# Moving small steps of a transformer layer between VectorE, GpSimd and ScalarE: the rotary product, the high halves and the pair sums

## The chip, the core and the metric

The kernel runs on one core of a Trainium2 chip. The metric is the device time of one execution, in microseconds. Before the change three runs gave 1519.38, 1523.75 and 1528.3 us; their median is 1523.75 us. The engines are called by the names of the profile: PE is TensorE (PEld its weight loads), DVE is VectorE, ACT is ScalarE, POOL is GpSimd, SP is the engine that issues most DMAs.

## The reference

The input x has 2 x 1024 rows of 1024 values, in f32. The reference computes one layer in three steps, each on a layer norm of what came before:

```
x = x + 0.5 * ffn(layernorm(x))
x = x + attention(layernorm(x))
x = x + 0.5 * ffn(layernorm(x))        # the same weights as the first ffn

ffn(x):       base = x @ base_w.T + base_b
              gate = top 2 of 8 experts by x @ gate_w.T, weights by softmax of the two
              low  = x @ lora_A[e].T            (rank 16, all 8 experts)
              base + 2 * sum_e gate[e] * low[e] @ lora_B[e].T
attention(x): q = x @ Wq (32 heads of 32), k = x @ Wk, v = x @ Wv (8 heads of 32)
              q, k = rotary(q), rotary(k):  q * cos + rotate_half(q) * sin
              softmax(causal(q k^T / sqrt(32))) v, four q heads to one k head, then @ Wo
```

## The kernel before

**Precision.** PE multiplies in f16. Each f32 operand is written as a high half (the value rounded to f16) and a low half (what is left, in f16), and a product is the sum of three matmuls: high by high, high by low, low by high (`dense`, L361 to L363). The halves are made on the vector engines. For a normed row tile this is `Split.add`: the high half is a copy (L311 on ACT for the first two tiles' first norm, L313 on POOL for all others), the low half a subtraction on DVE (L314), and a transposing DMA issued by SP brings both to the layout that PE needs (L317). For q and k the halves stand side by side in one tile, so that one matmul over 96 rows sums all three products: `kv_out` writes high, low and again high (L499 to L501), `q_out` high, high and low (L510 to L512), and the second high half is a DVE copy of the first.

**Tiles and stages.** There are 16 row tiles of 128 rows, 8 to a batch entry. Each passes through four stages: `stage_a1` (norm, first FFN, norm), `stage_a2` (k and v, then q in two parts, with the rotary step `rope`), the attention of its 8 key heads, `stage_c1` (output projection, norm) and `stage_c2` (second FFN, store). The base weights of the FFN stay on the chip; those of the attention are split once, written to DRAM (`wstr`) and streamed back in pieces by DMAs from SP (L373).

**The attention of a tile.** For each key head g, `unit_s1` makes scores of all 4 query heads against each key tile j (L575, three accumulators) and takes their row maxima on DVE (L592); the maxima are put into the query tile, and a transposing DMA (`qt_load`, L555) brings it to PE. `unit_s2` then makes the transposed scores (L695, two accumulators), and ACT takes the exponential (L701, tile `p32`, 8 buffers). For the diagonal tile POOL sets the masked part to zero (L703). The sums of two neighbouring exponentials (`pair`, L710, 2 buffers) serve the denominator. `av_add` collects up to `BATCH` = 4 exponentials; when `SKEW` = 2 further ones have been made, `av_batch` issues the batch's products with the values and with ones (L641, accumulator `av`). The last batch of a head is divided out by L648 to L657.

**Order.** The dense stages are Python generators that yield after every two steps of k, that is six matmuls. `step` runs the attention of a tile slot by slot, and after each slot takes dense pieces from the stages planned beside it, so many that `npieces` (from `SIZE`) are used up by the end of the tile; what is left over is issued at its end. The order of emission is a priority: a scheduler at build time places the instructions of each engine by it and by its own timing, and the engines run their queues strictly in that order. Two things bind it further: dense instructions stand on PE behind the score product some steps back (`behind`), and the matmuls of one batch in `av_batch` stand in a chain of their own. At the start, `piece`, `pow2` and `split` (L169 to L195) prepare the weights on ACT, DVE and POOL while the first tiles run.

**The lines that the change touches.** In `rope` ACT copies the accumulator to `qs` (L468), DVE makes the product with the cosine from `qs` (L472), POOL the two products with the sine (L477, L481), and DVE adds (L485). In `ffn` the accumulator of the base and expert products is finished by L445, and DVE adds it to the residual tile `xt` (L446). Two accumulators (`p_dense`) serve all dense products.

Of the kernel before, what the change touches and what calls it, by code (L numbers as in the profile page):

```python
# [19 lines left out]
P = 128  # L20
# [19 lines left out]
def kernel(  # L40
# [256 lines left out]
    class Split:  # L297
# [4 lines left out]
            self.tt = tp.tile([P, 2 * KB, P], HP, name="tt")  # L302
            self.n, self.done = n, 0

        def add(self, src, act=False):

            w, i = D // self.n, self.done
            src = src[:, i * w : (i + 1) * w]
            hi = self.hl[:, 2 * i * w : (2 * i + 1) * w]
            if act:  # L310
                nc.scalar.copy(hi, src)  # L311
            else:
                nc.gpsimd.tensor_scalar(hi, src, 1.0, 0.0, ALU.mult, ALU.add)  # L313
            nc.vector.tensor_tensor(self.hl[:, (2 * i + 1) * w : (2 * i + 2) * w], src, hi, ALU.subtract)  # L314
            m = 2 * KB // self.n
            pin(
                nc.sync.dma_start_transpose(  # L317
                    out=self.tt[:, i * m : (i + 1) * m, :], in_=self.hl[:, 2 * i * w : (2 * i + 2) * w]
                )
            )  # L320
            self.done += 1
# [6 lines left out]
            m = KB // self.n  # L328
            return self.tt[:, k // m * 2 * m + m + k % m, :]

    def layernorm(xt, act=False, n=1):
# [12 lines left out]
        rs = small.tile([P, 1], FP, name="rs")  # L344
        nc.vector.tensor_tensor(rs, n1, r, ALU.mult)
        nb = small.tile([P, 1], FP, name="nb")
        nc.vector.scalar_tensor_tensor(nb, mv[:, 0:1], -1.0, rs, ALU.mult, ALU.mult)
        xn = fpool.tile([P, D], FP, name="xn")
        sp = Split(n)
        for i in range(n):  # L350
            c = bass.ts(i, D // n)
            nc.scalar.activation(xn[:, c], xt[:, c], AF.Identity, bias=nb, scale=rs)
            sp.add(xn, act)
        return sp

    def dense(ps, tt, wsel, n=512, last=True):
# [36 lines left out]
    def ffn(xt, tt, done):  # L393
# [34 lines left out]
        for n in range(2):  # L428
# [14 lines left out]
            nc.tensor.matmul(ps, lhsT=lh, rhs=lbh[:, c], start=False, stop=False)  # L443
            nc.tensor.matmul(ps, lhsT=lh, rhs=lbl[:, c], start=False, stop=False)
            nc.tensor.matmul(ps, lhsT=ll, rhs=lbh[:, c], start=False, stop=True)  # L445
            nc.vector.scalar_tensor_tensor(xt[:, c], ps, S["uf", n], xt[:, c], ALU.mult, ALU.add)  # L446
            done(n)
            if n == 0:
                yield True

    def stage_a1(t):
        tt = layernorm(xts[t], t < 2)
        yield

        def done(n):
# [9 lines left out]
    def rope(ps, n, nh, i):  # L465
# [6 lines left out]
        nc.vector.tensor_tensor(  # L472
            t1.rearrange("p h (a d) -> p (h a) d", a=2),
            qs.rearrange("p h (a d) -> p (h a) d", a=2),
            cosT[:, i, :].unsqueeze(1).to_broadcast([P, 2 * nh, H]), ALU.mult,
        )
        nc.gpsimd.tensor_tensor(  # L477
            t2[:, :, 0:H], qs[:, :, H:DH],
# [11 lines left out]
    def kv_out(t, ps):  # L490
# [7 lines left out]
        ks = kst  # L498
        nc.scalar.copy(ks[:, :, 0:DH], k1)  # L499
        nc.vector.tensor_tensor(ks[:, :, DH : 2 * DH], k1, ks[:, :, 0:DH], ALU.subtract)  # L500
        nc.vector.tensor_copy(ks[:, :, 2 * DH : 3 * DH], ks[:, :, 0:DH])  # L501
        kt = kts[:, (t + TPB) % (TPB + 1)]
        nc.sync.dma_start_transpose(out=kt, in_=ks.rearrange("p g c -> p (g c)"))
        KT[t] = kt
# [1 line left out]
    def q_out(t, n, ps):  # L506
# [2 lines left out]
        h = slice(n * 16, n * 16 + 16)  # L509
        nc.scalar.copy(qs[:, h, 0:DH], q1)  # L510
        nc.vector.tensor_tensor(qs[:, h, 2 * DH : 3 * DH], q1, qs[:, h, 0:DH], ALU.subtract)
        nc.vector.tensor_copy(qs[:, h, DH : 2 * DH], qs[:, h, 0:DH])  # L512
# [99 lines left out]
    class Context:  # L612
# [8 lines left out]
        def low(self, k):  # L621
            return self.tt[:, KB + k, :]

    def av_batch():

        t, g, L, us = pend.popleft()
        if us[0][0] == 0:
            avt[0] = p_av.tile([P, 2, P], FP, name="av")
        av = avt[0]
        last = us[-1][0] == L - 1  # L630
        runs = [(0, VA[t - t % TPB + j][:, g, :], p32) for j, p32, _ in reversed(us)]
        runs += [(1, ones, sums) for _, _, sums in reversed(us) if sums is not None]
        prev = None
        for n, (i, w, p32) in enumerate(runs):
            for h in range(GRP):
# [22 lines left out]
            if g == NKV - 1:  # L658
                CT[t] = CTX.pop(t)

    def av_add(t, g, j, L, p32, sums):

        if not pend or len(pend[-1][3]) == BATCH or pend[-1][0:2] != (t, g):
            pend.append((t, g, L, []))
        pend[-1][3].append((j, p32, sums))
        after = 0
        while len(pend) > 1:
            after = sum(len(b[3]) for b in list(pend)[1:])
            if after < SKEW:
                break  # L670
            av_batch()
# [15 lines left out]
    def unit_s2(t, g):  # L687
# [5 lines left out]
        for j in range(L):  # L693
# [8 lines left out]
            if j == L - 1:  # L702
# [1 line left out]
                    out=p32, in_=p32, compare_op=ALU.is_ge, fill=0.0, base=0,  # L704
                    pattern=[[0, GRP], [1, P]], channel_multiplier=-1,
                )
            sums = None
            if j % 2 == 1:
                sums = pp.tile([P, GRP, P], FP, name="pair", bufs=2)
                nc.vector.tensor_tensor(sums, even, p32, ALU.add)  # L710
            elif j == L - 1:
                sums = p32
            even = p32
            av_add(t, g, j, L, p32, sums)
            yield

    def stage_c1(t):
# [312 lines left out]
```

## Time and profile before

| | |
|---|---|
| median of 3 runs | 1523.75 us (1519.38 to 1528.3) |
| profiled execution | 1522.31 us, of which the span from first to last instruction is 1520.5 us |
| mean granted clock of PE | 0.973 |
| busy: PE, DVE, ACT, POOL | 1396.4, 1182.2, 687.9, 518.3 us |
| instructions: PE, DVE, ACT, POOL | 14548, 2468, 1280, 711 |
| HBM | 181.63 MB read, 20.45 MB written, 133 GB/s over the span |

A busy time is the union of the instructions' own durations; an engine that waits in its queue for a semaphore is idle. Matmuls are pipelined and their ends are modelled, so a busy PE is not a PE at its peak. The clock is what the throttle granted to PE, as a share of full speed. The chain that ended last is followed back from the last instruction, at each step to what released it or to the instruction before it on its engine. Lines are those of the kernel before; durations of single groups come from the one profiled execution.

### The profile page before, as it was taken

How to read it: one execution, taken by the hardware profiler on the slowest of the kernel's cores; microseconds unless marked ns; L12 is line 12 of the kernel's file. 1: busy time of each engine (PE TensorE's matmuls, PEld its weight loads, DVE VectorE, ACT ScalarE, POOL GpSimd, SP SyncE). 2: the span in 40 equal slices, each digit the busy share in tenths (PEclk: the TensorE clock that was granted, in tenths of full speed). 3: DMA queues.
4: the chain of work that ended last, by engine and by line, in shares of the span. 5: the costliest groups of instructions: out<-in, count | busy, mean ns of one | idle time of the engine just before them, and what ended most of it. 6: DMA issues, size and time to landing. Idle time of an engine off the chain costs nothing.

```text
span 1520.5 us, 35288 instructions
## 1 busy us (share of the span) xinstructions
PE 1396.4 (92%) x14548; PEld 781.8 (51%) x14548; DVE 1182.2 (78%) x2468; ACT 687.9 (45%) x1280; POOL 518.3 (34%) x711
## 2 busy tenths in 40 slices
PE   3687699799999999998999899989999999999998
PEld 2343345465555555555644445545555555556544
DVE  6877668786969799688864777877879799799653
ACT  7453325353545445454542334433545445465530
POOL 3443224523424334132232434433424232321231
PEclk9898899999999999999999999999999999999999
DMA  9967778849383753834646769657483854923551
GB/s 278 309 180 156 159 242 213 259 118 298 72 290 76 220 169 57 271 98 85 212 143 193 216 198 267 174 150 245 95 279 66 232 151 85 270 71 85 133 174 42
DMA packets 293074, 267.29 MB, mean 176 GB/s; under 512 B 258480, under 2 KB 261552, under 8 KB 272432
## 3 DMA queue, kind: packets, MB, share of 16 engines
q1 hardware_dynamic: 289360, 252.45, 60.5%
q10 hardware_dynamic: 3552, 12.58, 2.4%
q8 instruction: 114, 1.87, 0.5%
q14 instruction: 48, 0.39, 0.1%
HBM read 181.63 MB, written 20.45 MB: 133 GB/s over the span
## 4 chain that ended last, share of the span: by engine, by line
PE 59%; DVE 18%; DMA 9%; issue 3%; POOL 3%; ACT 2%; SPq 1%; ACTq 0%; DVEq 0%; POOLq 0%
PE pd L361 12%; PE pd L362 12%; PE pd L363 12%; PE av L641 10%; PE s L695 6%; PE s L575 6%; DVE mx L592 5%; DMA ws<-wstr 4%; DMA qt<-qst 3%; DVE pair L710 3%; DVE hl L314 2%; DVE o L650 2%; DMA wstr<-ws 1%; ACT p L701 1%; DVE ws L195 1%
## 5 line engine op out<-in xcount | busy, mean ns | idle before, releaser
L701 ACT ACTIVATE p<-s,cs 128x512 f32<-128x512 f32 x576 | 381.3, 687 | 265.1 <-PE s L695 261.5
L592 DVE TENSOR_REDUCE mx<-s 128x4 f32<-128x512 f32 x480 | 314.6, 676 | 60.4 <-PE s L575 36.4
L575 PE MATMUL s<-kts,qt 96*128 96x128 f16 x2304 | 219.6, 222 | 25.4 <-DMA qt<-qst 12.7
L361 PE MATMUL pd<-ws,tt 128*128 128x512 f16 x592 | 225.9, 382 | 11.6 <-DMA ws<-wstr 9.5
L710 DVE TENSOR_TENSOR pair<-p,p 128x512 f32<-128x512 f32 x256 | 190.5, 747 | 56.3 <-ACT p L701 25.8
L695 PE MATMUL s<-qt,kts 128*128 128x512 f16 x576 | 210.9, 385 | 21.9 <-DMA qt<-qst 15.1
L575 PEld LDWEIGHTS <-qt 96*128 96x128 f16 x2304 | 166.9, 99 | 120.8 <-issue 35.7
L362 PE MATMUL pd<-ws,tt 128*128 128x512 f16 x592 | 225.7, 381 | 0.0
L363 PE MATMUL pd<-ws,tt 128*128 128x512 f16 x592 | 225.0, 381 | 0.0
L361 PE MATMUL pd<-wb,tt 128*128 128x512 f16 x512 | 197.4, 386 | 7.7 <-DVE xt L446 6.1
L362 PEld LDWEIGHTS <-tt 128*128 128x128 f16 x1360 | 134.5, 99 | 134.5 <-issue 26.2
L363 PEld LDWEIGHTS <-tt 128*128 128x128 f16 x1360 | 134.4, 99 | 129.1 <-issue 6.3
L361 PEld LDWEIGHTS <-tt 128*128 128x128 f16 x1360 | 134.6, 99 | 125.6 <-issue 16.3
L362 PE MATMUL pd<-wb,tt 128*128 128x512 f16 x512 | 196.9, 385 | 0.4 <-DVE wb L195 0.4
L363 PE MATMUL pd<-wb,tt 128*128 128x512 f16 x512 | 196.3, 383 | 0.0
L641 PE MATMUL av<-p,va 128*32 128x128 f32 x4608 | 167.2, 279 | 2.5 <-ACT o L648 1.9
L703 POOL TENSOR_SCALAR_AFFINE_SELECT p<-p 128x512 f32<-128x512 f32 x128 | 91.8, 720 | 226.0 <-ACT p L701 222.3
L657 POOL TENSOR_TENSOR tt<-o,tt 128x128 f16<-128x128 f32 x128 | 62.7, 490 | 277.2 <-ACT tt L656 266.9
L641 PEld LDWEIGHTS av<-p,va 128*32 128x32 f32 x4608 | 116.1, 110 | 62.3 <-issue 48.0
L650 DVE RECIPROCAL o<-o 128x128 f32<-128x128 f32 x128 | 120.6, 943 | 15.9 <-ACT o L648 15.7
L587 POOL TENSOR_SCALAR_AFFINE_SELECT sm<-sm 128x512 f32<-128x512 f32 x96 | 66.3, 690 | 139.5 <-ACT sm L586 136.9
L398 POOL TENSOR_TENSOR xt<-xt,bb 128x512 f32<-128x512 f32 x64 | 106.0, 1677 | 0.0
(178 smaller groups left out, 1840.0 us busy)
## 6 DMA issues: line engine op xcount, KB each, us to landing
ws<-wstr SPq DMA_DIRECT2D x148, 1024.0 KB, 5.8
wstr<-ws ACTq DMA_DIRECT2D x9, 1024.0 KB, 6.5
xt<-in_x_dram SPq DMA_DIRECT2D x16, 512.0 KB, 4.5
out_dram<-xt SPq DMA_DIRECT2D x15, 512.0 KB, 2.7
ws<-in_wb_dram SPq DMA_DIRECT2D x2, 1024.0 KB, 8.0
qst<-in_wb_dram SPq DMA_DIRECT2D x2, 1024.0 KB, 7.5
st<-in_wo_dram SPq DMA_DIRECT2D x2, 1024.0 KB, 11.2
kts<-in_wo_dram SPq DMA_DIRECT2D x2, 1024.0 KB, 12.3
```

The source lines that it names most:

```text
L361: nc.tensor.matmul(ps, lhsT=th, rhs=wh, start=(k == 0), stop=False)
L362: nc.tensor.matmul(ps, lhsT=th, rhs=wl, start=False, stop=False)
L363: nc.tensor.matmul(ps, lhsT=tl, rhs=wh, start=False, stop=(last and k == KB - 1))
L398: nc.gpsimd.tensor_tensor(xt[:, c], xt[:, c], bb[:, c], ALU.add)
L575: nc.tensor.matmul(ps[:, h, :], lhsT=q[0 : 3 * DH, h, :], rhs=KT[b0 + j][0 : 3 * DH, g, :], start=(not pem or h == 0), stop=not pem,)
L592: nc.vector.tensor_reduce(mx[:, odd, j, :], ps, AX.X, ALU.max)
L641: prev = nc.tensor.matmul(av[rows, i, :], lhsT=w, rhs=p32[:, h, :], start=(us[0][0] == 0 and n == 0), stop=(last and n == len(runs) - 1), ...
L650: nc.vector.reciprocal(rc, rc)
L695: ins = nc.tensor.matmul(ps.rearrange("p h k -> p (h k)"), lhsT=KT[b0 + j][:, g, :], rhs=q.rearrange("p h k -> p (h k)"), start=True, stop ...
L701: nc.scalar.activation(p32, ps, AF.Exp, scale=cs)
L703: nc.gpsimd.affine_select(out=p32, in_=p32, compare_op=ALU.is_ge, fill=0.0, base=0, pattern=[[0, GRP], [1, P]], channel_multiplier=-1,)
L710: nc.vector.tensor_tensor(sums, even, p32, ALU.add)
```

## The change

Five things are changed, and the computed function stays the same.

1. In `Split.add` the high half is always copied by ACT; the choice of the engine (`act`) is gone.
2. In `rope` the cosine product reads the accumulator itself and scales by 2^-23 in the same DVE instruction. ACT's scaled copy `qs` stays for the sine products.
3. In `kv_out` and `q_out` the second high half is an ACT copy of the rotated product, in place of a DVE copy of the first high half.
4. The pair sums are no longer made right after their second exponential. `add_pairs` makes all sums of a batch together, when the first exponential of the next batch has been made, or at the latest in `av_batch`. An odd exponential at the end of a head goes to the denominator by itself, as before.
5. In `ffn` there is a `yield` more, between the last expert matmul and the residual update, for each of the two halves. The counts in `SIZE` are as before.

No edges of order are added for any of this.

```diff
-        def add(self, src, act=False):
+        def add(self, src):
...
-            if act:
-                nc.scalar.copy(hi, src)
-            else:
-                nc.gpsimd.tensor_scalar(hi, src, 1.0, 0.0, ALU.mult, ALU.add)
+            nc.scalar.copy(hi, src)
             nc.vector.tensor_tensor(self.hl[:, (2 * i + 1) * w : (2 * i + 2) * w], src, hi, ALU.subtract)
...
             nc.tensor.matmul(ps, lhsT=ll, rhs=lbh[:, c], start=False, stop=True)
+            yield
             nc.vector.scalar_tensor_tensor(xt[:, c], ps, S["uf", n], xt[:, c], ALU.mult, ALU.add)
...
-        nc.vector.tensor_tensor(
+        nc.vector.scalar_tensor_tensor(
             t1.rearrange("p h (a d) -> p (h a) d", a=2),
-            qs.rearrange("p h (a d) -> p (h a) d", a=2),
-            cosT[:, i, :].unsqueeze(1).to_broadcast([P, 2 * nh, H]), ALU.mult,
+            ps.rearrange("p (h a d) -> p (h a) d", a=2, d=H), 2.0**-23,
+            cosT[:, i, :].unsqueeze(1).to_broadcast([P, 2 * nh, H]), ALU.mult, ALU.mult,
         )
...
-        nc.vector.tensor_copy(ks[:, :, 2 * DH : 3 * DH], ks[:, :, 0:DH])
+        nc.scalar.copy(ks[:, :, 2 * DH : 3 * DH], k1)
...
-        nc.vector.tensor_copy(qs[:, h, DH : 2 * DH], qs[:, h, 0:DH])
+        nc.scalar.copy(qs[:, h, DH : 2 * DH], q1)
...
+    pairs = {}
+
+    def add_pairs(batch):
+
+        t, g, L, us = batch
+        key = (t, g, us[0][0])
+        if key in pairs:
+            return
+        pairs[key] = []
+        for i in range(0, len(us), 2):
+            if i + 1 == len(us):
+                pairs[key].append(us[i][1])
+                continue
+            sums = pp.tile([P, GRP, P], FP, name="pair", bufs=2)
+            nc.vector.tensor_tensor(sums, us[i][1], us[i + 1][1], ALU.add)
+            pairs[key].append(sums)
+
     def av_batch():
 
+        add_pairs(pend[0])
         t, g, L, us = pend.popleft()
...
-        runs += [(1, ones, sums) for _, _, sums in reversed(us) if sums is not None]
+        runs += [(1, ones, sums) for sums in reversed(pairs.pop((t, g, us[0][0])))]
...
         while len(pend) > 1:
             after = sum(len(b[3]) for b in list(pend)[1:])
+            add_pairs(pend[0])
             if after < SKEW:
                 break
             av_batch()
...
-            sums = None
-            if j % 2 == 1:
-                sums = pp.tile([P, GRP, P], FP, name="pair", bufs=2)
-                nc.vector.tensor_tensor(sums, even, p32, ALU.add)
-            elif j == L - 1:
-                sums = p32
-            even = p32
-            av_add(t, g, j, L, p32, sums)
+            av_add(t, g, j, L, p32)
             yield
```

More of the change, by code (lines that the diff above doesn't have):

```diff
@@ L329, in low, with layernorm @@
             return self.tt[:, k // m * 2 * m + m + k % m, :]
-    def layernorm(xt, act=False, n=1):
+    def layernorm(xt, n=1):
         st = small.tile([P, 2, 6], FP, name="bst")
@@ L352, in layernorm @@
             nc.scalar.activation(xn[:, c], xt[:, c], AF.Identity, bias=nb, scale=rs)
-            sp.add(xn, act)
+            sp.add(xn)
         return sp
@@ L451, in stage_a1 @@
     def stage_a1(t):
-        tt = layernorm(xts[t], t < 2)
+        tt = layernorm(xts[t])
         yield
@@ L630, in av_batch @@
         last = us[-1][0] == L - 1
-        runs = [(0, VA[t - t % TPB + j][:, g, :], p32) for j, p32, _ in reversed(us)]
-        runs += [(1, ones, sums) for _, _, sums in reversed(us) if sums is not None]
+        runs = [(0, VA[t - t % TPB + j][:, g, :], p32) for j, p32 in reversed(us)]
+        runs += [(1, ones, sums) for sums in reversed(pairs.pop((t, g, us[0][0])))]
         prev = None
@@ L659, in av_batch, with av_add @@
                 CT[t] = CTX.pop(t)
-    def av_add(t, g, j, L, p32, sums):
+    def av_add(t, g, j, L, p32):
         if not pend or len(pend[-1][3]) == BATCH or pend[-1][0:2] != (t, g):
             pend.append((t, g, L, []))
-        pend[-1][3].append((j, p32, sums))
+        pend[-1][3].append((j, p32))
         after = 0
```

## The prediction

> **What bounds the kernel now.** I read four views. First the page: busy time of each engine, and the chain that ended last.
>
> ```profile
> PE 1396.4 (92%) x14548; PEld 781.8 (51%) x14548; DVE 1182.2 (78%) x2468; ACT 687.9 (45%) x1280; POOL 518.3 (34%) x711
> ...
> PE 59%; DVE 18%; DMA 9%; issue 3%; POOL 3%; ACT 2%; SPq 1%; ACTq 0%; DVEq 0%; POOLq 0%
> ```
>
> PE is the engine that the end waits for, with DVE second: 18% of the chain is 274 us (0.18 x 1520.5), while ACT, on which the change puts work, carries 2% (30 us). Next the windows of 100 us (columns: busy of PE, PEld, DVE, ACT, POOL, then granted clock), because the 8% that PE lacks is not spread evenly.
>
> ```profile
> 0.00:100.00 100.00, 62.79 (x307) 32.08 (x308) 75.60 (x203) 59.32 (x94) 39.18 (x74) 0.90 0.91 270
> 100.00:200.00 100.00, 73.40 (x524) 36.60 (x523) 71.67 (x161) 38.01 (x70) 36.89 (x49) 0.86 0.70 148
> ...
> 400.00:500.00 100.00, 98.96 (x1142) 56.82 (x1135) 84.68 (x171) 49.72 (x93) 39.88 (x50) 1.00 0.58 162
> ```
>
> The first 200 us lack 64 us of PE, at a granted clock of 0.90 and 0.86; in the middle PE is at 99% and nothing that happens on DVE or ACT can be worth much there. Third, what PE itself waited for (engine, line, releaser: total us, times, longest).
>
> ```profile
> PE s L575 <- DVE mx L592: 12.1, 21, 3.4
> ...
> PE s L695 <- ACT p L701: 6.4, 12, 2.1
> PE pd L361 <- DVE xt L446: 6.3, 3, 3.6
> PE s L436 <- DVE lw L421: 5.8, 3, 3.0
> ...
> PE av L641 <- DVE pair L710: 3.3, 8, 1.4
> ```
>
> The whole list comes to about 119 us; 27 us of it are DVE's attention and expert work above, 28 are the query transposes (`DMA qt<-qst`, 15.1 and 12.7), 9.5 the streamed weights, 33 the scale set-up at the start (L174 and L445 on L179, untouched). So what a lighter DVE can give is bounded by some 30 us plus what hangs behind it. Fourth, the groups by line and shape (busy us, mean ns, idle before it and its releasers), for the prices.
>
> ```profile
> L701 ACT ACTIVATE p<-s,cs 128x512 f32<-128x512 f32 x576 | 381.3, 687 | 265.1 <-PE s L695 261.5 <-DVE pair L710 0.7 <-POOL p L703 0.6
> L710 DVE TENSOR_TENSOR pair<-p,p 128x512 f32<-128x512 f32 x256 | 190.5, 747 | 56.3 <-ACT p L701 25.8 <-PE av L641 20.7 <-POOL p L703 9.5
> L314 DVE TENSOR_TENSOR hl<-xn,hl 128x1024 f16<-128x1024 f32 x48 | 81.8, 1704 | 13.3 <-POOL hl L313 13.3
> L313 POOL TENSOR_SCALAR hl<-xn 128x1024 f16<-128x1024 f32 x46 | 50.3, 1093 | 91.2 <-ACT xn L352 91.2
> L446 DVE SCALAR_TENSOR_TENSOR xt<-pd,uf,xt 128x512 f32<-128x512 f32 x64 | 46.9, 737 | 24.8 <-PE pd L445 24.4
> L472 DVE TENSOR_TENSOR t<-qs,cosT 128x512 f32<-128x512 f32 x32 | 30.7, 959 | 28.1 <-ACT qs L468 28.1
> L510 ACT CAST qst<-t 128x512 f16<-128x512 f32 x32 | 19.8, 617 | 55.2 <-DVE t L485 54.9
> L311 ACT CAST hl<-xn 128x1024 f16<-128x1024 f32 x2 | 2.1, 1028 | 0.0
> L512 DVE COPY qst<-qst 128x512 f16<-128x512 f16 x32 | 12.7, 398 | 0.0
> ```
>
> **The sum, part by part.** I weigh a cut on an engine by that engine's share of the chain, because DVE's work is mostly beside PE: one us off DVE is worth 0.18 us on average. All against the profiled run, 1522.3 us (span 1520.5, 1.8 around it); the median of the runs, 1523.75, lies 1.4 above it.
>
> *Copies of high halves to ACT.* Off DVE go 32 x 398 ns (L512) and 16 x 219 ns (L501): 16.2 us. On ACT come 32 x 617 (as L510) and 16 x 403 (as L499): 26.1 us. The second copy reads the rotated product and not the first copy, so DVE's subtraction at L511 runs beside it; the transposes need both, so the chain keeps one operation less on DVE and gets one more on ACT.
>
> *Cosine product from the accumulator.* L472 takes 959 ns (512 wide) and 509 (256 wide): 38.9 us. The nearest row of the new form, one accumulator operand and one in SBUF, is L446 with 737. For 256 wide I interpolate between 128 wide (L421, 284) and 512 wide: an estimate of 435. That makes 32 x 737 + 16 x 435 = 30.6 us, 8.3 less; at worst no gain. It no longer waits for ACT's copy (28.1 us of DVE idle before it), but POOL's two sine products still do, and the sum at L485 waits for them (13.2 us now): what is late next is POOL, so I count no latency gain.
>
> *High halves of layer norms to ACT.* POOL loses 46 x 1093 = 50.3 us, ACT gets 46 x 1028 = 47.3. In the chain norm, high, low, transposes the step is 65 ns shorter (3 us in all, and one hand-over between engines less): 1 us on the path. The low half that follows on DVE (L314) takes 1704 ns in the mean: 1212 is the median of the 13 that have no POOL instruction beside them in the trace, 2279 of the 27 that lie mostly beside one. POOL's bias adds (L398, 106 us) remain and now start earlier, so of the 48 x (1704 - 1212) = 24 us I take 5, with 0 and 24 as ends. The Trainium skill ("SBUF — State Buffer", section "SBUF: two separate sides") says that a VectorE instruction with two SBUF inputs and a GpSimd instruction that reads SBUF lock each other out for a whole instruction; by it alone the bias adds would go on blocking the low halves and this term would be zero.
>
> DVE together: 16.2 + 8.3 + 5 = 29.5 us, 2.5% of 1182; times the 274 us of DVE in the chain: **-6.8 us** (ends -3.7 and -11).
>
> *Pair sums with their batch.* The 256 sums stay, at 747 ns; what goes is that one stands at the head of DVE's queue waiting for an exponential just issued (25.8 us) or for a buffer that the batch before still holds (20.7 us), with score maxima queued behind it. Of these 46.5 us I take 40 away. Lower bound: the scheduler places the sums as before (in the built programs the same 49 of 256 stand behind a maximum whose scores come later), and nothing goes; upper bound all of it. At 0.18: **-7 us** (0 to -8). The context product now waits for two sums made at once, 1.5 us; it has its own distance of two units, so that is hidden; without that cover each of 256 would cost up to 0.7.
>
> *ACT's queue.* ACT rises by 73.4 us to 761 (50% of the span). By its chain share (30.4 x 10.7%): **+3.2 us**. The floor is zero: ACT idles 265 us before the exponentials. The ceiling is 46 times an extra 1.03 us in front of an exponential in a third of the cases: +15. The Trainium skill ("ScalarE: Activation LUTs", section "Rules for kernel authors") advises VectorE for simple elementwise work; the rows agree on price (398 against 617 ns per copy), and by that rule alone this move would be a loss of 10 us of engine time.
>
> *Accumulator held until DVE is done.* The product now reads the accumulator, so its release waits for DVE as well as ACT. Per eviction PE waited 6.3/64 = 0.10 us on DVE's (L446) and 1.0/48 = 0.02 on ACT's. 48 x 0.08 = 3.8, rounded down for the few tiles in a row: **+3 us** (0 to 5).
>
> *The added yield in the FFN.* The residual update is issued one slot later; each FFN chunk has one piece more at an unchanged pace, so a few pieces of 6 x 216 ns move to the end of each step. PE keeps working there: **+1** (0 to 4).
>
> *Start.* In the built order the exponential of one early gate (L405) stands behind about twelve weight splits (L194, near 0.5 us each) that it preceded before, and the gate's copy `lh` behind more. The splits come earlier in exchange: 0, with ends -5 and +6.
>
> Sum: -6.8 - 7 - 1 + 3.2 + 3 + 1 = -7.6. The clock adds to it: 2.7% of the clock is lost, 41 us, and the low windows are those in which PE waited; 7.6 of 119 us of waits less gives -3. So -10.6: 1511.7 on the profiled run, **1513** on the median.
>
> **Rivals.** *ACT's queue decides (slower).* Each layer norm now occupies ACT for 1238 + 1028 = 2.27 us instead of 1.24, and in the built order 14 of 48 have nothing between the two. The score product for the context has two accumulators; PE stops when an exponential is more than about two units late. For it: PE already waits 6.4 us on L701, and these waits are few and long. Against it: ACT idles half the time, and exponentials stand between in the other cases. If every second norm stops PE for one high half, 24 us are lost; with the other terms (-10.8 without ACT's 3.2) that is +13, and with the clock in the same proportion +18: 1541. It decides from the point where PE's wait for L701 passes 25 us.
>
> *Hidden anyway.* From 300 to 600 us and from 1100 to 1300 PE is at 97 to 99%; if DVE's part of the chain is only where an equally late alternative stands beside it, -7.6 shrinks to -2: 1521.
>
> *More at the start.* If the first 200 us, where DVE is busy 72 to 76% and on the chain with splits and low halves, take 12 of the 64 missing us back: 1501.
>
> That the change doesn't do what it says is ruled out by the built order: 46 fewer POOL operations, 48 fewer on DVE, 94 more on ACT, matmuls the same.
>
> **Chances.** Forecast 0.34, more at the start 0.10, hidden 0.22, ACT's queue 0.30, other slowdowns 0.04. A difference under 0.5% (7.6 us) is what a measurement of this kernel can't tell from none. Faster by more than that 0.44, within 0.22, slower 0.34. The range: all gains at their ends (-11 - 8 - 1 - 5, with clock -34) give 1490, the rival's 1541 with the start's +6 gives 1547: 1490 to 1547. The forecast's own range, between the two other cases without a loss, is 1503 to 1516.
>
> **What would show it.** Right: DVE near 1153 us, POOL near 468, ACT near 761; `t<-pd` at 650 to 740 ns; idle before the pair sum under 25 us; PE's waits on the maxima under 9 us; the clock above 0.973. Wrong: PE's wait on the exponential over 15 us, PE waiting on the cosine product over 5 us, or a first 200 us with less PE work than 136 us. If DVE falls as said and the span does not, the chain share was the wrong weight.

## The result: no change in time, and the profile after

The changed kernel takes 1522.22 us (median of 20 runs, 1516.88 to 1529.27), the kernel before 1524.3 us (20 runs, 1517.56 to 1529.26). The ratio is 0.9991, with a 95% interval from 0.9977 to 1.0005. A gain of a few microseconds can't be excluded, the forecast ten can: the lower end is 3.5 us. The time is the one that the rival "hidden anyway" named (1521).

The profiled execution of after took 1528.7 us (span 1527.0), 6.5 above its median, and that of before 1.9 below its own. So differences of a few microseconds between the two profiles' totals mean nothing; the groups can be compared, the waits with some care. The page's busy line and chain by engine, of after:

```profile
PE 1404.1 (92%) x14548; PEld 783.4 (51%) x14548; DVE 1139.7 (75%) x2420; ACT 755.5 (49%) x1374; POOL 450.1 (29%) x665
...
PE 65%; DVE 13%; DMA 13%; ACT 3%; issue 2%; POOL 1%; SPq 1%; DVEq 0%; ACTq 0%; POOLq 0%
```

The work moved as the change says: DVE 42.5 us less, POOL 68.2 less, ACT 67.6 more. DVE's share of the chain fell from 18% to 13%, and DMA's rose from 9% to 13%. The same windows as before (PE, PEld, DVE, ACT, POOL, granted clock, DMA share, GB/s), of after:

```profile
0.00:100.00 100.00, 62.26 (x293) 31.22 (x294) 74.88 (x209) 60.48 (x94) 35.12 (x70) 0.88 0.88 270
100.00:200.00 100.00, 79.00 (x550) 39.50 (x549) 71.00 (x153) 44.96 (x83) 33.89 (x48) 0.91 0.65 151
200.00:300.00 100.00, 86.21 (x775) 44.39 (x777) 60.94 (x133) 42.09 (x84) 31.01 (x50) 0.97 0.80 225
300.00:400.00 100.00, 94.03 (x943) 55.05 (x932) 76.14 (x150) 47.29 (x91) 34.93 (x47) 0.95 0.70 197
400.00:500.00 100.00, 97.35 (x1139) 56.63 (x1137) 79.83 (x178) 51.39 (x98) 32.26 (x48) 1.00 0.61 162
...
600.00:700.00 100.00, 98.59 (x1241) 58.91 (x1240) 82.12 (x166) 57.24 (x101) 28.68 (x38) 1.00 0.58 161
```

Three windows of before, to set beside these:

```profile
200.00:300.00 100.00, 91.01 (x820) 47.15 (x818) 76.32 (x152) 41.40 (x83) 47.33 (x63) 0.99 0.85 257
300.00:400.00 100.00, 97.18 (x1034) 57.17 (x1038) 80.93 (x178) 45.70 (x89) 32.07 (x48) 0.97 0.64 173
...
600.00:700.00 100.00, 93.30 (x1127) 55.72 (x1125) 81.92 (x163) 46.29 (x84) 27.79 (x39) 0.97 0.59 166
```

The first 200 us have 5 us more of PE work (141.3 against 136.2), and from 600 to 700 us there are 5 us more (98.6 against 93.3). From 200 to 400 us there are 8 us less (180.2 against 188.2). So the change did gain in places, and lost it again in another. What PE waited for, of after (total us, times, longest):

```profile
PE s L573 <- DMA qt<-qst: 17.8, 10, 5.7
PE pd L358 <- DMA ws<-wstr: 16.8, 15, 2.2
PE s L712 <- DMA qt<-qst: 11.6, 12, 2.1
PE s L433 <- DVE lw L418: 11.4, 6, 4.6
...
PE pd L358 <- DMA tt<-hl: 6.1, 5, 2.1
PE s L573 <- DVE mx L590: 5.7, 15, 0.9
PE pd L358 <- DVE xt L444: 5.3, 4, 4.8
PE s L712 <- ACT p L718: 4.3, 11, 1.2
```

PE's waits for DVE come to 52.1 us (67.7 before), those for DMAs to 52.3 (40.2 before), and all of them to 117.5 against 118.8. This reads as if a transfer now held up what DVE no longer did, but the totals alone don't show it. Over half of the 15.6 us less for DVE (8.6) lies in the first 200 us, where the waits of the scale set-up, which the change doesn't touch, are shorter (L174 on `sq`: 18.6 before, 9.6 after). And the list differs from one profile to the next: that of `pairs_only` below, where every queue holds the same order as in the kernel before, has 45.9 us for DMAs and 122.9 in all.

Behind the first 200 us, the waits for DVE went from 20.2 to 13.1 us and those for DMAs from 27.6 to 37.5. The wait on the maxima was halved (12.1 to 5.7), as predicted; the one on the streamed weights rose from 9.5 to 16.8 (it is 13.7 in `pairs_only`, and 16.3 with parts 1 to 3 alone), and the rise lies between 200 and 460 us (2.9 to 10.3), where PE work is missing. The wait on the query transposes stayed (16.7 and 16.4). That fits a second bound, DMA, beside DVE; the experiments test it.

The groups of after, by line and shape (busy us, mean ns, idle before and its releasers):

```profile
L636 DVE TENSOR_TENSOR pair<-p,p 128x512 f32<-128x512 f32 x256 | 185.6, 727 | 72.6 <-ACT p L718 34.8 <-PE av L657 22.3 <-POOL p L720 14.1
L311 DVE TENSOR_TENSOR hl<-xn,hl 128x1024 f16<-128x1024 f32 x48 | 65.5, 1364 | 17.9 <-ACT hl L310 17.9
L310 ACT CAST hl<-xn 128x1024 f16<-128x1024 f32 x48 | 50.1, 1044 | 0.4
L470 DVE SCALAR_TENSOR_TENSOR t<-pd,cosT 128x512 f32<-128x512 f32 x32 | 21.9, 685 | 24.8 <-ACT qs L466 24.4
L510 ACT CAST qst<-t 128x512 f16<-128x512 f32 x32 | 19.7, 614 | 0.0
L395 POOL TENSOR_TENSOR xt<-xt,bb 128x512 f32<-128x512 f32 x64 | 92.3, 1464 | 59.6 <-ACT xn L349 59.4
```

The low half takes 1364 ns where it took 1704, the cosine product 685 where it took 959, the two moved copies 1044 and 614 ns on ACT. The idle time before the pair sum did not fall: 72.6 us, against 56.3.

### The profile page after: what moved, and what is told of

The parts are those of the page before. It is cut to its first block, busy times and chain, and to the rows that moved or that the text cites. A ratio compares the mean times of both kernels' runs of the same rounds, so it can differ in the third digit from the quotient of the medians.

```text
span 1527.0 us, 35303 instructions
## 1 busy us (share of the span) xinstructions
PE 1404.1 (92%) x14548; PEld 783.4 (51%) x14548; DVE 1139.7 (75%) x2420; ACT 755.5 (49%) x1374; POOL 450.1 (29%) x665
## 4 chain that ended last, share of the span: by engine, by line
PE 65%; DVE 13%; DMA 13%; ACT 3%; issue 2%; POOL 1%; SPq 1%; DVEq 0%; ACTq 0%; POOLq 0%
PE pd L358 13%; PE pd L359 13%; PE pd L360 13%; PE av L657 10%; PE s L712 7%; PE s L573 6%; DMA ws<-wstr 6%; DMA qt<-qst 5%; DVE mx L590 3%; DVE pair L636 1%; DVE ws L195 1%; DMA tt<-hl 1%; DVE o L666 1%; ACT p L718 1%; DVE hl L311 1%
## 5 line engine op out<-in xcount | busy, mean ns | idle before, releaser
L718 ACT ACTIVATE p<-s,cs 128x512 f32<-128x512 f32 x576 | 382.3, 688 | 291.2 <-PE s L712 284.1
L358 PE MATMUL pd<-ws,tt 128*128 128x512 f16 x592 | 226.8, 383 | 20.9 <-DMA ws<-wstr 16.8
L636 DVE TENSOR_TENSOR pair<-p,p 128x512 f32<-128x512 f32 x256 | 185.6, 727 | 72.6 <-ACT p L718 34.8
L712 PE MATMUL s<-qt,kts 128*128 128x512 f16 x576 | 210.7, 386 | 16.4 <-DMA qt<-qst 11.6
L358 PEld LDWEIGHTS <-tt 128*128 128x128 f16 x1360 | 135.6, 100 | 135.5 <-issue 16.7
L360 PE MATMUL pd<-wb,tt 128*128 128x512 f16 x512 | 197.7, 386 | 0.0
L673 POOL TENSOR_TENSOR tt<-o,tt 128x128 f16<-128x128 f32 x128 | 70.5, 551 | 279.6 <-ACT tt L672 279.3
L395 POOL TENSOR_TENSOR xt<-xt,bb 128x512 f32<-128x512 f32 x64 | 92.3, 1464 | 59.6 <-ACT xn L349 59.4
```

Source lines behind the costliest of these rows:

```text
L358: nc.tensor.matmul(ps, lhsT=th, rhs=wh, start=(k == 0), stop=False)
L360: nc.tensor.matmul(ps, lhsT=tl, rhs=wh, start=False, stop=(last and k == KB - 1))
L395: nc.gpsimd.tensor_tensor(xt[:, c], xt[:, c], bb[:, c], ALU.add)
L636: nc.vector.tensor_tensor(sums, us[i][1], us[i + 1][1], ALU.add)
L712: ins = nc.tensor.matmul(ps.rearrange("p h k -> p (h k)"), lhsT=KT[b0 + j][:, g, :], rhs=q.rearrange("p h k -> p (h k)"), start=True, stop ...
L718: nc.scalar.activation(p32, ps, AF.Exp, scale=cs)
```

## Experiments

Each ratio is to the kernel before, run beside it (its median was 1521.5 to 1523.4 in the five sets). Theory A is the one of the prediction, an engine's microsecond weighed by its share of the chain; the rivals are ACT's added queue eating the gain, and a second bound, DMA, taking DVE's place. One thing holds for all comparisons: a build places the instructions of each engine anew, so each kernel also has an order of its own.

### Which part does anything, with the transposes in place

`engines_only` has parts 1 to 3 of the change, `pairs_only` part 4.

> Parts 1 to 3 alone (high halves, cosine product, second copies), pair sums and FFN as before. Cancelling theory (the moves gain what the prediction said and the pair sums or the added yield take it back): 1515 or faster. Hidden theory: 1519 to 1528, with DVE's busy time near 1140 as in the whole change. ACT's queue as a loss: over 1530.

> Part 4 alone on the kernel before. The prediction's step: the idle time of DVE before the pair sum falls from 56 us to under 25 and the time by 7 us, to 1517. Hidden theory, from the profile of the whole change (72.6 us of idle before the sum): the idle time stays at 50 to 80 us and the time within 4 us. Cancelling theory: 1530 or slower.

Measured: 1522.96 us, ratio 1.0001 [0.9981, 1.0020], with DVE at 1141.9 us; and 1522.39 us, 0.9993 [0.9975, 1.0012]. So parts 1 to 3 together bring nothing beyond some 3 us, and nor does part 4; a gain of one group doesn't hide a loss of the other. The whole change has parts 4 and 5 more than `engines_only`: its ratio is 0.0010 lower, uncertain by 0.0024, so the yield (part 5) brings no more than a few microseconds either way. By the prediction's own terms parts 1 to 3 sum to -1.6 us without the clock (-6.8 - 1 + 3.2 + 3), which this run can't tell from nothing. In the groups of `pairs_only` the sum's stall is where it was:

```profile
L638 DVE TENSOR_TENSOR pair<-p,p 128x512 f32<-128x512 f32 x256 | 189.5, 744 | 57.2 <-ACT p L720 26.7 <-PE av L659 20.7 <-POOL p L722 9.7
```

57.2 us, of which 26.7 behind the exponential, against 56.3 and 25.8. The traces say why: by operation and tiles, all 2468 instructions of DVE stand in the same order as in the kernel before, and so do those of PE, ACT and POOL and the DMAs of SP. The scheduler puts the sums into DVE's queue as before, wherever the program writes them. So `pairs_only` is in effect the kernel before once more.

### Does more on ACT, or more on DVE, cost what its share says?

```diff
 # before_act: five small copies after each norm's activation, 240 in all, 218 ns each
+            jk = small.tile([P, 32], FP, name="jk", bufs=1)
+            for _ in range(5):
+                nc.scalar.copy(jk, xt[:, 0:32])
 # before_dve: two spare statistics per norm behind the aggregate, ahead of `ve`
+        jk = small.tile([P, 2, 6], FP, name="jk")
+        for c in range(2):
+            nc.vector.bn_stats(jk[:, c, :], xt[:, bass.ts(c, 512)])
 # before_dve_late, after_dve_late: the same lines behind sp.add(xn)
```

> The kernel before with five small ACT copies into a tile that nobody reads behind each norm (240 in all, an estimate of 0.23 us each from the row of the 128x8 activations, 0.27): some 55 us of ACT work, in blocks of over 1 us behind the 1.24 us of the norm, as the change puts there. ACT's queue as a rival: each second block stops PE, 24 us slower, about 1548. Chain share as a weight: 30.4 x 55/688 = 2.4 us slower. Hidden theory: within 4 us, PE's wait on the exponential (L701) under 12 us.

> The kernel before with the two statistics instructions of each layer norm made a second time into a tile that nobody reads: 96 more DVE instructions of 0.685 us, 66 us of DVE work on no chain of data. Chain share as a weight (the prediction's step): 0.18 x 66 = 12 us slower, about 1536. Hidden theory (DVE's queue has idle time to give, PE's waits change their names only): within 4 us of the kernel before, with PE's waits on the maxima (L592) under 20 us. If DVE is nearer to the bound than both say, over 20 us slower.

> The kernel before with the same 96 spare statistics instructions, but issued behind the norm's low half, so that no step of the norm waits for them: 66 us of DVE load and no longer chain. If DVE's load is what cost 58 us in the first try (where they stood between the statistics and their aggregate), again 40 us or more slower. If the length of the norm's chain is what counts, within 8 us of the kernel before.

> The changed kernel with the same 96 spare DVE instructions behind the low half: DVE at 1140 + 66 = 1206 us of work, against 1248 in the kernel before with the same addition. If the change has made room on DVE that the kernel does not use, this is within 8 us of the kernel before, and faster than the kernel before with the same load. If load is hidden in both, both are within 8 us. If it is no better than the other, the change gave nothing that DVE needs.

Measured: `before_act` 1526.4 us, 1.0019 [1.0000, 1.0038], ACT at 731.5 us. Some 44 us more on ACT cost 3 us, by the interval none or up to 6: this work of ACT's, put behind the norms, is not dear. `before_dve` 1582.41, 1.0381 [1.0354, 1.0409]; `before_dve_late` 1582.47, 1.0399 [1.0367, 1.0431]. The spare work is 96 x 676 ns = 65 us, and it costs 59 and 61 us: 0.9 us per us, five times the 0.18 that theory A gives, though in the second form nothing of the norm's own chain waits for it directly. (In the first form it stands behind the aggregate, not between the statistics and the aggregate, as the expectation of the second says.) The chain of `before_dve_late`:

```profile
PE 53%; DVE 26%; DMA 11%; issue 3%; POOL 2%; ACT 2%; SPq 1%; POOLq 0%; DVEq 0%; ACTq 0%
```

DVE's share grew to 26%: a share tells what is on the chain now, not what 65 us at one place would add. Part of it may be the clock: the mean granted clock over the runs fell from 0.972 to 0.961. Taken over the whole span (0.011 x 1521) that is an estimate of 17 of the 61 us; that the longer waits brought the clock down isn't shown. `after_dve_late`: 1571.57, 1.0329 [1.0302, 1.0355], some 50 us above the changed kernel. Its DVE is busy 1185.9 us, as the kernel before's (1182.2), and it is 50 us slower than that. The sum of DVE's work doesn't set the time, its place does. But with the same spare work in both, the changed kernel is 11 us faster than the kernel before (1571.57 against 1582.47, in one set, and the intervals don't meet), transposing DMAs and all. So the change does make room on DVE, and the room counts once DVE has more to do at the norms.

`before_pool_lat` makes the small POOL step `ve` of the norm six times, some 50 us of POOL in all and 1.4 us more in the chain of each norm; `before_norecip` leaves the reciprocal of the denominator out (the context is multiplied by the denominator, so the result is another), 121 us of DVE instructions in the attention, 0.94 us of them in the chain at the end of each head.

```diff
 # before_pool_lat
-        nc.gpsimd.tensor_scalar(ve, mv[:, 1:2], EPS, None, ALU.add)
+        for _ in range(6):
+            nc.gpsimd.tensor_scalar(ve, mv[:, 1:2], EPS, None, ALU.add)
 # before_norecip
-            nc.vector.reciprocal(rc, rc)
```

> The kernel before with the norm's small POOL step (variance plus epsilon, L338, 0.29 us) made six times in a row instead of once: the norm's chain is 5 x 0.29 = 1.4 us longer, as in the first try, and DVE has nothing more to do. Length of the chain: 40 us or more slower. Load of DVE: within 6 us.

> The kernel before without the reciprocal of the denominators (L650; the context is multiplied by the denominator instead, so this part of the computation is changed): 121 us less on DVE, 0.94 us less in the chain at the end of each head. Chain share as a weight: 0.18 x 121 = 22 us faster, 1502. Hidden theory: within 6 us, since what PE waits for next (the query transposes, the streamed weights) does not come earlier.

Measured: 1558.37, 1.0245 [1.0214, 1.0277]: 50 to 67 us of added latency in 48 norms (POOL's busy time grew by 50.6 us, the forecast sum is 67) cost 37 us, with DVE's load nearly unchanged (1189.4 us) and the clock at 0.965. So a longer chain of steps in the norm costs as well, without more work on DVE. And 1500.79, 0.9865 [0.9838, 0.9891]: the reciprocals' 121 us bring 21 us, 0.17 per us of instruction time. DVE's busy time fell by only 86.3 us (1182.2 to 1095.9), because its instructions overlap in the trace and others took longer; by that it is 0.24. The shorter chain at the end of a head is in the same 21 us. Near theory A's weight, then, and DVE's work is not hidden as a whole.

### Are the transposing DMAs the second bound?

The DMAs that PE waits for more in the changed kernel come from SP's queue. Every split norm and every pair of key heads issues a transposing DMA there. In the plain kernels all 192 of them are plain copies of the same bytes into the same tiles, so the layout is not the one that the products need, and the kernels compute something else; the scales are lowered to keep the numbers finite, which changes no instruction's shape.

```diff
-            nc.sync.dma_start_transpose(out=q, in_=QS[t][:, g*GRP:(g+2)*GRP, :].rearrange(...))
+            nc.sync.dma_start(out=q, in_=QS[t][:, g*GRP:(g+2)*GRP, :])
 # the same for tt and kt
-  2.0**26 / (DH**0.5)          1.0 / MROW
+  2.0**-60 / (DH**0.5)         2.0**-100
```

> The kernel before with its 192 transposing DMAs replaced by plain copies of the same size (the transposes are left out, and the exponent's scale and the maxima are scaled to nearly zero to keep values finite, so the attention and the dense products are changed); engines' work is the same, instruction for instruction. Its PE no longer waits for transposes (28 us of query transposes, 3 of norms in the kernel before), if those were slow by their transposing: 20 to 40 us faster, 1485 to 1505. If their issue, late behind the maxima on SP, was what PE waited for: within 8 us of the kernel before. It is the base for the next three.

> The changed kernel with the same plain copies. Theory 'what DVE gave went into waits for DMA': with the transposes short, the change shows, 6 us or more faster than the plain kernel before. Theory 'given back on ACT and in order': within 4 us of it. ACT's queue as a loss that DMA waits covered: 6 us or more slower.

Measured: `plain_before` 1514.58 us, 0.9933 [0.9910, 0.9956]; `plain_after` 1497.44, 0.9819 [0.9793, 0.9845]. The kernel before gains 9 us by the plain copies, less than the 20 to 40 that were expected if PE waited for slow transposes. But with plain copies the change that brought nothing brings 17.1 us, 1.1%, and the intervals don't meet. The issues on SP's queue (ns least, median, most; first and last start), two lines of the kernel before:

```profile
L317 SPq DMA_TRANSPOSE tt<-hl x48: 1317/2039/7259, 15.8 to 1498.9; - x48
L555 SPq DMA_TRANSPOSE qt<-qst x128: 1231/1288/5497, 126.9 to 1444.0; - x128
```

The same two of `plain_before`:

```profile
L317 SPq DMA_DIRECT2D tt<-hl x48: 464/465/1142, 15.8 to 1492.7; - x48
L556 SPq DMA_DIRECT2D qt<-qst x128: 464/471/1842, 137.3 to 1440.0; - x128
```

A transposing issue holds SP's queue 2.7 and 4.4 times as long as a plain one (1288 against 471 ns, 2039 against 465). Summed with the key transposes it is 372 us of SP's span before and 102 us plain, and the streamed weights stand behind them in the same queue. The transfers differ too: the query DMA lands after 3.6 us at the median before and 2.5 in `plain_before`, the DMA share from 400 to 500 us is 0.58 and 0.44, and the same 267 MB move in 293,074 packets before and in 68,818 there. What PE waited for in `plain_before`:

```profile
PE s L574 <- DVE mx L591: 16.8, 22, 3.4
...
PE pd L362 <- DMA ws<-wstr: 8.4, 8, 1.7
PE s L694 <- DMA qt<-qst: 7.5, 6, 3.7
```

and in `plain_after`:

```profile
...
PE s L572 <- DVE mx L589: 5.6, 13, 0.9
PE pd L359 <- DMA ws<-wstr: 5.2, 7, 2.0
...
PE s L711 <- DMA qt<-qst: 4.8, 4, 2.3
```

The wait on the maxima falls by 11 us (6 with the transposes), and the DMAs don't take their place: PE's waits for DMAs go from 26.8 to 18.9 us, where with the transposes they went from 40.2 to 52.3. All its waits fall from 114.6 to 96.6, about the gain. Behind the first 200 us they fall from 54.4 to 34.0: 6.4 us less for DVE, 8.1 for DMAs, 4.6 for ACT and 1.3 for POOL. The windows show where (us of PE work in each stretch, from one profile each; `pairs_only` and `plain_pairs_only`, the two kernels before once more, are within 2.1 us of them in every row):

| stretch, us | before | after | `plain_before` | `plain_after` |
|---|---|---|---|---|
| 0 to 200 | 136.2 | 141.3 | 139.8 | 137.1 |
| 200 to 400 | 188.2 | 180.2 | 184.3 | 188.9 |
| 400 to 600 | 196.3 | 195.3 | 195.2 | 195.2 |
| 600 to 800 | 190.0 | 196.5 | 190.8 | 197.7 |
| 800 to 1100 | 285.0 | 281.8 | 286.1 | 291.2 |

From 600 to 800 us the change gains the same with and without transposes, some 7 us, and there the wait on the maxima goes (from 600 to 760 us: 4.9 to 0.8, and 5.0 to 0.6). What differs is 200 to 400 and 800 to 1100 us: with the transposes the changed kernel loses PE work there, with plain copies it gains. (In `engines_only` the loss lies from 400 to 600 us, 190.8, so it isn't tied to one place.) From 200 to 460 us PE's wait on the streamed weights rises from 2.9 to 10.3 us in the first case and is 3.2 and 2.5 in the second. The chain of `plain_after` shows it in shares:

```profile
PE 73%; DVE 14%; DMA 5%; ACT 3%; issue 3%; POOL 2%; SPq 0%; ACTq 0%; DVEq 0%; POOLq 0%
```

### Which part of the change the gain is

With plain copies, parts 1 to 3, part 4, all but part 1, part 2 alone and part 3 alone:

> Parts 1 to 3 alone (high halves, cosine product, second copies), with plain copies for the transposing DMAs. If the 17 us that the change gives there come from the lighter DVE: 12 us or more faster than the plain kernel before (1503 or less). If they come from the pair sums or the yield: within 4 us of it.

> Part 4 alone (pair sums with their batch), with plain copies. The prediction's step (-7 us): 1508. From the profiles, where the idle time before the pair sum does not fall: within 4 us of the plain kernel before, 1511 to 1519.

> The changed kernel with part 1 undone (high halves of the norms on POOL again, but for the first two), with plain copies. If what DVE gains from POOL's silence and the shorter hand-over counts (its low half takes 1364 ns in place of 1704): 5 us or more slower than the plain changed kernel. If ACT's 47 us are the dearer side: 4 us or more faster.

> Part 2 alone (cosine product from the accumulator), with plain copies. With part 1 undone the plain changed kernel keeps its 17 us, so parts 2 and 3 hold them. By DVE work (some 9 of 26 us, with the contention that it escapes): 4 to 9 us faster than the plain kernel before. If the hand-over from ACT's copy is what counts: 12 us or more.

> Part 3 alone (second copies of the high halves on ACT), with plain copies. By DVE work (16 of 26 us): 8 to 13 us faster than the plain kernel before. If the chain from the rotary product to the load of q is what counts (ACT's second copy runs beside DVE's subtraction, where DVE's copy came behind it): 12 us or more. If neither part alone gives 5 us, the gain is of the order built with both.

| kernel | us | ratio | difference from `plain_before`, us | DVE busy |
|---|---|---|---|---|
| `plain_engines_only` | 1495.27 | 0.9817 [0.9792, 0.9841] | -18 | 1139.6 |
| `plain_pairs_only` | 1512.51 | 0.9936 [0.9913, 0.9959] | 0 | 1185.7 |
| `plain_after_hi_pool` | 1496.22 | 0.9827 [0.9804, 0.9851] | -16 | 1167.1 |
| `plain_cos_only` | 1499.54 | 0.9849 [0.9821, 0.9877] | -13 | 1171.6 |
| `plain_copies_only` | 1502.59 | 0.9877 [0.9849, 0.9905] | -9 | 1175.1 |

The kernels stem from different sets, so the difference is that of the two ratios times 1522 us; each is uncertain by some 5 us.

`plain_pairs_only` has the same order in every queue as `plain_before`, so it is that kernel measured again. The high halves on ACT are worth nothing here (1496.22 without that part, 1497.44 with it), though that part takes the most off DVE and POOL. The gain is in the two edits of the rotary step and its query and key halves: 13 us for 14 of DVE, 9 us for 10, and 16 for the 18 of both. That is about 0.9 us per us of DVE, four to five times what the share of the chain (18 and 20%) would give; with 5 us of uncertainty on each it is no price to carry elsewhere, though the two add up within it. Nor is it shown that the load is what counts. By its expectation (4 to 9 us for DVE's work, 12 or more for the hand-over) the 13 us of part 2 speak for the hand-over, and its rotary step is shorter too: from the start of ACT's copy to the end of the sum it takes 3.57 us at the median, in `plain_before` 3.98. The 9 us of part 3 lie where DVE's work was expected. And as the table shows, the gain lies in a few stretches of the run and not with every tile.

Last, the cost of ACT's work and of DVE's at two places, with plain copies. `plain_after_noact` copies only 8 of the 1024 columns of each high half after the first two norms, and leaves out the second copies of q and k.

```diff
 # plain_after_noact
-            nc.scalar.copy(hi, src)
+            m8 = w if full[0] <= 2 else 8
+            nc.scalar.copy(hi[:, 0:m8], src[:, 0:m8])
-        nc.scalar.copy(ks[:, :, 2 * DH : 3 * DH], k1)
-        nc.scalar.copy(qs[:, h, DH : 2 * DH], q1)
 # plain_before_dve_att: spare statistics in unit_s2, behind the exponential
+            if j == 0 and g < 6:
+                jk = small.tile([P, 6], FP, name="jk")
+                nc.vector.bn_stats(jk, p32.rearrange("p h k -> p (h k)"))
```

> The plain changed kernel without most of what the change put on ACT: the high half of a norm copies 8 of 1024 columns (all only in the first two norms), and the second high halves of q and k are left out, so this part of the computation is changed too. ACT loses some 64 us, the norm's chain 0.8 us in each of 46 cases, DVE keeps its lower load. Theory 'given back on ACT and in the chain': at least 8 us faster than the plain changed kernel. Theory 'hidden': within 4 us of it.

> The plain kernel before with 96 spare DVE statistics instructions of 0.685 us (66 us), not at the norms but in the attention, one behind the first exponential of six heads in eight. If DVE's load costs the same everywhere: 50 us or more slower than the plain kernel before, as at the norms in the kernel with transposes. If the norm is a place of its own and the attention pays the chain share (0.17, as the missing reciprocals gave): 8 to 16 us slower.

> The plain kernel before with the 96 spare DVE instructions (66 us) at the norms, behind the low half, which cost 60 us with transposing DMAs. If a late norm costs so much because its transposing DMA then stands in SP's queue among the weight loads: under 25 us slower than the plain kernel before. If DVE at the norms is tight by itself: 45 us or more slower, as before, against 7 for the same load in the attention.

Measured: 1488.52, 0.9755 [0.9729, 0.9781], 8.9 us below `plain_after`: a ceiling on what ACT's added work costs, since the norm's chain is also shorter by a copy. `plain_before_dve_att` 1521.92, 0.9988 [0.9972, 1.0003]: 7.3 us for 65 us of DVE in the attention, 0.11 per us. `plain_before_dve_late` 1547.28, 1.0156 [1.0130, 1.0181]: 34 us over `plain_before` (by the ratios) for the same 65 us at the norms, where it was 61 with the transposes. The same work costs between four and five times as much at the norms as in the attention, and nearly twice as much again when the transposing DMAs come behind it. The 34 us lie between the two readings of the expectation (under 25, 45 or more): both DVE's place at the norms and the transposes behind it have a part.

## Why the prediction was wrong, by its steps

**Which steps failed.** The sum was -7.6 us, with -3 for the clock on top. In it the pair sums have -7, parts 1 to 3 together -1.6 and the yield +1. So nearly the whole forecast hung on the pair sums, and these gave nothing. The second failure is the price of the -6.8 for DVE's work: one us off DVE at the chain's 0.18, whatever the place and whatever else ends beside it.

**The pair sums' -7** failed outright. Part 4 alone leaves every queue in the order of the kernel before, the idle time before the sum at 57.2 us (56.3 before), and the time where it was (0.9993, and 0.9936 against 0.9933 with plain copies). The idle time of 72.6 us in the whole change comes with the other parts. The prediction named this case as its lower bound (the built order keeps the same sums in front) and then took the other end: the queue's built order was evidence, the program's was not.

**DVE's work** came out larger than costed: 42.5 us off and not 29.5. The copies went as listed, ACT rose by 67.6 us where 73.4 was taken, and the cosine product takes 685 ns where 737 was taken. The low halves were mis-sized: 48 x (1704 - 1364) = 16.3 us, where 5 was chosen between 0 and 24. The Trainium skill ("SBUF — State Buffer", "SBUF: two separate sides") says that of such a VectorE and GpSimd pair whichever starts first keeps the other out for the whole instruction. The trace agrees: where a bias add of POOL's runs when a low half starts, the low half ends 1.08 us after the add's end at the median, before and after. The prediction's zero was the rule put to the wrong times: the adds no longer wait for POOL's copy, but for ACT's `xn` (59.4 us), so 12 of them start over 1 us ahead of the low half, which then takes 1.32 us, where 20 started under 0.7 us ahead before and it took 2.28. The cosine product gained in a similar way: 16 of the 32 before took 0.68 to 0.69 us from SBUF, as all do from the accumulator now (0.67 to 0.69), and the other 16 took 0.84 to 1.76 us, with POOL instructions beside them all the time.

**The weight.** The signs that it gave for its own error came: DVE fell more than said and the span did not. A uniform 0.18 for DVE was near for the reciprocal (0.17), and wrong for the norms (0.9). For parts 1 to 3 it gave -1.6 us with ACT's and the accumulator's terms: too little to tell from the 0 measured with the transposes, and far from the -18 measured with plain copies. The waits on the maxima fell under 9 us as predicted. The prediction listed 28 us for the query transposes and 9.5 for the streamed weights, and treated them as fixed and separate; the waits for DMAs behind the first 200 us grew by 10 us as those for DVE shrank by 7, most of it on the weights. That is "hidden anyway", with DMA as the equally late alternative, as far as the lists go; that the transposing DMAs are needed for it is shown by the runs without them, but for what the order of a build may add.

**ACT's queue**, the rival on the slow side, was wrong: PE's wait on the exponential fell from 6.4 to 4.3 us, and `before_act` puts 44 us at 3, 6 at the most. The rule of the Trainium skill ("ScalarE: Activation LUTs", "Rules for kernel authors"), VectorE before ScalarE for simple elementwise work such as add and mul, holds here for the price of a copy (398 against 617 ns); as a rule for where to put it, it would have kept these copies on VectorE, and `plain_copies_only` gains 9 us, uncertain by 5, by moving them. **Accumulator held** (+3): the trace after lists no wait of PE for the cosine product above 1.0 us. The cosine product still idles 24.4 us behind ACT's `qs`, which it doesn't read any more; the releaser in the row is inferred. **Start**: 5 us more of PE work, inside the ends given, but 8 us less in the 200 us behind it. **Clock** (-3): 0.974 against 0.973 in the profiled executions. Over its 20 runs the changed kernel has 0.976, where the kernel before has 0.972 in each of the five sets; the time is the same all the same, and why isn't shown.

**What stays open.** That the change is worth 17 us once the transposing DMAs are plain is shown: four programs with rotary edits have ratios of 0.9817 to 0.9849, one (the copies alone) 0.9877, and the one without any, measured twice, 0.9933 and 0.9936. It is only one program without, though, and each build has an order of its own; how much of the 17 us belongs to that order wasn't tested. Which property of the transposes takes the gain is not separated: the longer hold on SP's queue, the later landing, the packets and the larger DMA share all went at once. No run made the streamed weights smaller, and parts 1 to 3 were not run one by one with the transposes in place, so a loss of one of them under a gain of another can't be excluded there. No version with the transposes in place and the same function was faster than both kernels, so none is offered.

## What to carry to other kernels

Before an engine's saved microseconds are weighed by its share of the chain, look at the place: put a known amount of spare work there on the chip and see what it costs, and list what else ends within a microsecond or two of the wait that will go. Where two resources end side by side, as DVE and the DMAs in SP's queue do here, relieving one may give nothing until the other is relieved too. Where a scheduler places the instructions, a gain from a different order has to be read from the built order, not from the program: here one of the five edits left every queue as it was. And before a list of waits is compared with another, see how far two profiles of the same program differ: here 40 and 46 us in the waits for DMAs.

## What the runs showed of the hardware

- A transposing DMA of the query halves holds SP for 1.29 us at the median and that of a norm tile for 2.04 (up to 7.3), against 0.47 us for plain copies of the same bytes. The query DMA lands after 3.6 us, the plain one after 2.5.
- The price of 65 us of instructions on DVE was 61 us at the norms with transposing DMAs behind them, 34 with plain ones, and 7 in the attention.
- The slower kernels have the lower mean clock: 0.977 when the reciprocal is left out (1500.8 us), 0.972 before, 0.965 and 0.961 with the longer norms (1558.4 and 1582.5 us). But the changed kernel has 0.976 at the time of the kernel before.
- A DVE subtraction of 128x1024 takes 1.21 us alone, and 2.28 where a POOL addition started up to 0.7 us ahead of it; started 1 us ahead, the addition costs it 0.11 us. The cosine product of 512 takes 0.68 us in either form where no POOL instruction is beside it.
